# A hand-written order from the first instruction on, edge lists along it, output transposes later, and part of p v on ScalarE, in a graph attention kernel

## Chip, core and metric

The kernel runs on one core of a Trainium2 chip. The metric is the device time of one execution in microseconds (us), as the median of several runs. The engines are TensorE (PE, with its weight loads as PEld), VectorE (DVE), ScalarE (ACT), GpSimd (POOL) and SyncE (SP). Each works through its own queue in order.

## What is computed

One layer of graph attention with a residual and a layer norm, over 16 batches of 1024 nodes with 512 features, 8 heads of 64. The adjacency matrix is the same for all batches and sparse.

```python
q = (x @ Wq + bq).reshape(b, n, H, HD)      # H = 8, HD = 64
k = (x @ Wk + bk).reshape(b, n, H, HD)
v = (x @ Wv + bv).reshape(b, n, H, HD)
scores = jnp.einsum('bqhd,bkhd->bhqk', q, k) / jnp.sqrt(jnp.float32(HD))
scores = scores + (1.0 - adj)[None, None, :, :] * -1000000000.0
attn = jax.nn.softmax(scores, axis=-1)
out = jnp.einsum('bhqk,bkhd->bqhd', attn, v).reshape(b, n, d)
x = _layernorm(x + out @ Wo + bo, axis=-1)  # x: (16, 1024, 512), adj: (1024, 1024)
```

All arithmetic is in 32-bit floats.

## The kernel before

Because the graph is sparse, the kernel works on edges. The 1024 queries are eight tiles of 128, and the edges of a tile are laid into blocks of 128 edges: 11, 6, 4, 4, 3, 3, 3 and 3 blocks, 37 in a batch and 592 in all.

*Edge lists.* `edges(t)` is a generator that makes, once for all batches, the list of a tile. It loads 128 rows of the adjacency (512 KB, from SP's queue), GpSimd multiplies them by column numbers, and VectorE takes out eight columns a round with a MAX (L284) and masks them (L286): ten rounds for tile 0, two for each other tile. Small matmuls (`poff` L295, `pe` L317) place the edges in blocks; the results are `key_row` and `query_row`, the row numbers to be gathered, and `sums`, a 0/1 matrix for each block, which comes out of transposes (`pof` L335).

*Products of a batch.* `front(b, t)` makes q, k and v of a tile from a transposed x (`transpose_x`, L356): each product is four 128x512 matmuls (L374), here called four units. q and kv go to DRAM as rows (`q_rows`, `kv_rows`, two buffers of each, so that one batch is written while another is read), and norms of q and k are collected on the way (squares on ScalarE L385, sums on VectorE L386). When the last tile is done, `mean_v` takes the mean of v by a matmul (`pm`), writes it behind the rows and sets `set_up[b]`; from then on the batch may be gathered.

*Blocks.* For block n, `gather` issues two indirect DMAs from GpSimd (q rows L495, kv rows L500), up to eight blocks ahead. `scores` multiplies q and k on VectorE (L509) and sums by head (L511), `exponentials` runs on ScalarE (L516), `weigh` multiplies v by the eight exponentials on VectorE (L520), and `add_up` adds the block to its queries by two matmuls with `sums` (L532, L533). Behind the last block of a tile `normalise` divides (o, L544), four transposes (`poT`, L553) turn the result, ScalarE copies it (oT), and the tile counts as done.

*Output.* `load_y` loads x again for a tile that is done, GpSimd adds the bias (L455), and `finish` multiplies by Wo (`po`, four units), adds y (L462), takes the layer norm's statistics (L465 to L468), the root on GpSimd (L471 to L473), scales on ScalarE (L476) and stores (L477). The loads of x and y and all stores stand in SP's queue in the order in which they are written.

*What sets the order.* Up to the first block a scheduler places the instructions: the lists of tiles 0 and 1, the bias products and all of batch 0's products. From there on the order is the one in which the program writes them (`tc.manual_schedule`). A loop over steps n puts into step n: the gathers up to n + 8, `weigh(n + 1)`, `scores(n + 2)`, what was put off to this step by `later(k, ...)`, `exponentials(n + 2)`, `add_up(n)`, and then units of other work for a credit of `share`, 3.165 a step (a unit costs 0.86, a group of transposes 0.44): first the units of the next batch's products, and only when these are used up the output products of tiles that are done. The lists of tiles 2 to 7 start at steps 1, 5, 9, 12, 15 and 18 and take one stage a step. Line numbers here and below are those of the kernel before.

## Time and profile before

| | us |
|---|---|
| median of 3 runs | 2704.92 (2704.65 to 2707.9) |
| the profiled execution | 2707.88 |
| its span, first to last instruction | 2706.1 |
| busy in the span: PE / DVE / ACT / POOL | 2507.0 / 2004.2 / 614.3 / 1531.2 |
| granted TensorE clock, mean | 0.966 |

The span cut into 40 equal slices of 67.7 us shows where each engine is busy; a digit is the busy share of a slice in tenths (9 is 90% or more), and the fifth row is the granted clock of TensorE in tenths of full speed:

```profile
PE   4978989999999999999999999999999999999866
PEld 2434545555555555555555555555554555555433
DVE  6358867777787777878777787867777787777775
ACT  2223222222222222222222222222222222222111
POOL 1055564746556474656647475564746566474773
PEclk8988999999999999999999999999999999999878
DMA  3266688787878878787888878787787878788773
```

PE is full in the middle, not in the first five slices and not in the last two. There its clock is below full speed as well.

### The profile page before, as it was taken

How to read it: one execution, taken by the hardware profiler on the slowest of the kernel's cores; microseconds unless marked ns; L12 is line 12 of the kernel's file. 1: busy time of each engine (PE TensorE's matmuls, PEld its weight loads, DVE VectorE, ACT ScalarE, POOL GpSimd, SP SyncE). 2: the span in 40 equal slices, each digit the busy share in tenths (PEclk: the TensorE clock that was granted, in tenths of full speed). 3: DMA queues.
4: the chain of work that ended last, by engine and by line, in shares of the span. 5: the costliest groups of instructions: out<-in, count | busy, mean ns of one | idle time of the engine just before them, and what ended most of it. 6: DMA issues, size and time to landing. Idle time of an engine off the chain costs nothing.

```text
span 2706.1 us, 26468 instructions
## 1 busy us (share of the span) xinstructions
PE 2507.0 (93%) x7659; PEld 1376.4 (51%) x7659; DVE 2004.2 (74%) x3655; ACT 614.3 (23%) x1428; POOL 1531.2 (57%) x1717
## 2 busy tenths in 40 slices
PE   4978989999999999999999999999999999999866
PEld 2434545555555555555555555555554555555433
DVE  6358867777787777878777787867777787777775
ACT  2223222222222222222222222222222222222111
POOL 1055564746556474656647475564746566474773
PEclk8988999999999999999999999999999999999878
DMA  3266688787878878787888878787787878788773
GB/s 124 89 225 230 229 276 270 254 275 250 285 252 281 267 255 275 245 286 253 282 262 267 265 248 288 251 279 263 265 272 237 284 254 286 264 271 252 237 264 112
DMA packets 228679, 678.02 MB, mean 251 GB/s; under 512 B 29454, under 2 KB 29466, under 8 KB 228524
## 3 DMA queue, kind: packets, MB, share of 16 engines
q0 software_dynamic: 132608, 465.64, 54.9%
q1 hardware_dynamic: 93344, 205.60, 20.1%
q10 hardware_dynamic: 2572, 4.99, 0.5%
q8 instruction: 63, 1.03, 0.2%
q14 instruction: 92, 0.75, 0.1%
HBM read 541.86 MB, written 134.25 MB: 250 GB/s over the span
## 4 chain that ended last, share of the span: by engine, by line
PE 71%; DVE 13%; POOL 7%; issue 6%; DMA 2%; ACT 1%; SPq 0%; POOLq 0%; DVEq 0%; ACTq 0%
PE pv L374 16%; PE pk L374 14%; PE pq L374 14%; PE po L374 8%; PE sum L533 7%; PE sum L532 7%; POOL kvg L500 3%; DVE pv L520 3%; DVE qg L509 2%; PE pxT L356 2%; DVE y L462 2%; DVE stats L465 2%; POOL qg L495 2%; PE poT L553 2%; DVE s L511 2%
## 5 line engine op out<-in xcount | busy, mean ns | idle before, releaser
L495 POOL DMA_INDIRECT qg<-q_rows,query_row x592 | 589.1, 995 | 781.0 <-DVE s L511 558.4
L500 POOL DMA_INDIRECT kvg<-kv_rows,key_row x592 | 592.0, 1000 | 194.4 <-issue 192.9
L520 DVE TENSOR_TENSOR pv<-kvg,pv 128x512 f32<-128x512 f32 x592 | 431.9, 730 | 265.5 <-ACT pv L516 236.4
L374 PE MATMUL pv<-wv,xT 128*128 128x512 f32 x1024 | 488.2, 606 | 0.3 <-DVE q L394 0.3
L374 PE MATMUL pk<-wk,xT 128*128 128x512 f32 x1024 | 479.3, 597 | 4.5 <-ACT kv L407 4.5
L374 PE MATMUL pq<-wq,xT 128*128 128x512 f32 x1024 | 482.0, 597 | 0.0
L374 PE MATMUL po<-wo,oT 128*128 128x512 f32 x1024 | 469.6, 599 | 0.0
L509 DVE TENSOR_TENSOR qg<-qg,kvg 128x512 f32<-128x512 f32 x592 | 427.0, 721 | 11.6 <-DMA kvg<-kv_rows,key_row 11.6
L511 DVE TENSOR_REDUCE s<-qg 128x8 f32<-128x512 f32 x592 | 406.2, 686 | 20.5
L532 PE MATMUL sum<-pv,sums 128*128 128x256 f32 x1184 | 368.8, 394 | 26.1 <-DVE pv L520 26.1
L533 PE MATMUL sum<-pv,sums 128*128 128x264 f32 x1184 | 374.3, 399 | 0.0
L516 ACT ACTIVATE pv<-s 128x8 f32<-128x8 f32 x592 | 124.4, 210 | 1082.3 <-DVE s L511 636.9
L532 PEld LDWEIGHTS sum<-pv,sums 128*128 128x128 f32 x1184 | 218.0, 196 | 237.8 <-issue 193.6
L374 PEld LDWEIGHTS pv<-wv,xT 128*128 128x128 f32 x1024 | 201.1, 196 | 205.8 <-issue 195.0
L374 PEld LDWEIGHTS pk<-wk,xT 128*128 128x128 f32 x1024 | 196.1, 192 | 208.7 <-issue 195.1
L374 PEld LDWEIGHTS po<-wo,oT 128*128 128x128 f32 x1024 | 196.9, 193 | 190.3 <-issue 178.6
L374 PEld LDWEIGHTS pq<-wq,xT 128*128 128x128 f32 x1024 | 187.8, 192 | 144.2 <-issue 136.1
L533 PEld LDWEIGHTS sum<-pv,sums 128*128 128x128 f32 x1184 | 232.9, 197 | 34.0
L462 DVE TENSOR_TENSOR y<-po,y 128x512 f32<-128x512 f32 x128 | 87.9, 687 | 152.5 <-POOL y L455 105.8
L455 POOL TENSOR_TENSOR y<-y,bo_bc 128x512 f32<-128x512 f32 x128 | 164.7, 1287 | 57.2 <-DMA y<-in_x_dram 50.9
L553 PE MATMUL poT<-ident,o 128*128 128x128 f32 x512 | 86.4, 293 | 109.5 <-DVE o L544 105.1
L386 DVE TENSOR_REDUCE nrm<-sq 128x8 f32<-128x512 f32 x256 | 172.0, 676 | 12.0 <-ACT sq L385 12.0
(97 smaller groups left out, 1624.0 us busy)
## 6 DMA issues: line engine op xcount, KB each, us to landing
kv_rows<-kv SPq DMA_DIRECT2D x128, 512.0 KB
x<-in_x_dram SPq DMA_DIRECT2D x128, 256.0 KB
q_rows<-q SPq DMA_DIRECT2D x128, 256.0 KB
y<-in_x_dram SPq DMA_DIRECT2D x128, 256.0 KB
out_dram<-y SPq DMA_DIRECT2D x128, 256.0 KB
qg<-q_rows,query_row POOLq DMA_INDIRECT x592
kvg<-kv_rows,key_row POOLq DMA_INDIRECT x592
a<-in_adj_dram SPq DMA_DIRECT2D x8, 512.0 KB
```

The source lines that it names most:

```text
L374: nc.tensor.matmul(p, lhs()[:, ts(c, P)], w[:, c, :], start=(c == 0), stop=(c == NPAIR - 1))
L386: later(1, lambda: nc.vector.tensor_reduce(NRM[b][:, i, t, :], sq.rearrange("p (h d) -> p h d", d=HD), axis=AX.X, op=OP.add))
L455: later(2, lambda: nc.gpsimd.tensor_tensor(Y[b, t], Y[b, t], bo_bc, op=OP.add))
L462: nc.vector.tensor_tensor(y, p, y, op=OP.add)
L495: nc.gpsimd.indirect_dma_start(out=QG[n], out_offset=None, in_=q_rows[b % 2], in_offset=bass.IndirectOffsetOnAxis(ap=query_row[:, g:g + 1] ...
L500: nc.gpsimd.indirect_dma_start(out=KG[n], out_offset=None, in_=kv_rows[b % 2], in_offset=bass.IndirectOffsetOnAxis(ap=key_row[:, g:g + 1], ...
L509: nc.vector.tensor_tensor(m, m, KG[n][:, 0:D], op=OP.mult)
L511: nc.vector.tensor_reduce(S[n], m.rearrange("p (h d) -> p h d", d=HD), axis=AX.X, op=OP.add)
L520: nc.vector.tensor_tensor(pv[:, 0:D].rearrange("p (h d) -> p h d", d=HD), v[:, D:].rearrange("p (h d) -> p h d", d=HD), pv[:, D:, None].to ...
L532: nc.tensor.matmul(SUM[b, t][:, 0, 0:HD2], m, pv[:, 0:HD2], **kw)
L533: nc.tensor.matmul(SUM[b, t][:, 1, 0:HD2 + HEADS], m, pv[:, HD2:], **kw)
L553: nc.tensor.transpose(p[:, ts(c, P)], o[:, ts(c, P)], ident)
```

## The change

The instructions and their sizes stay, but for a part of `weigh`. There are five edits.

1. The hand-written order starts at the first instruction, at step -34, and nothing is left to the scheduler. A step below 0 carries a share of 3.45, with the products of batch 0 and then of batch 1. `later` always puts off.
2. The edge lists start at steps -34, -16, -12, -8, -4, 0, 5 and 10, with one round of MAX and mask a step. The bias products are a generator too, from step -26 on.
3. The share of a step is worked out at each batch's start: all units that are left, over 37 steps. In a middle batch it is 3.07.
4. The transposes `poT` and the mean's matmul go into a list, `urgent`. A step empties it behind its `add_up` and, where product units of a batch are left, behind its first unit.
5. In batch 0 every odd block, and in batch 15 two blocks of three, have `weigh` on ScalarE: eight activations of 128x64, each with one head's exponential as its scale.

```diff
-EDGES_FROM = (0, 0, 1, 5, 9, 12, 15, 18)
+LEAD_IN = 34
+EDGES_FROM = (-34, -16, -12, -8, -4, 0, 5, 10)
+LEAD_SHARE = 3.45
...
         def later(k, fn):
-            if now[0] is None:
-                fn()
-            else:
-                plan.setdefault(now[0] + k, []).append(fn)
+            plan.setdefault(now[0] + k, []).append(fn)
...
                     nc.vector.scalar_tensor_tensor(
                         v, v, kl[:, r * 8 + 7:r * 8 + 8], v, op0=OP.is_lt, op1=OP.mult
                     )
+                    yield
...
             def mean_v():
+                urgent.append(mean_pe)
+
+            def mean_pe():
                 p = fill_psum(f"pm_{b}")
...
         def weigh(n):
             v, pv = KG.pop(n), PV[n]
+            b, t, i = blocks[n]
+            if (b == 0 and n % 2) or (b == B - 1 and n % 3):
+                for h in range(HEADS):
+                    nc.scalar.activation(
+                        pv[:, ts(h, HD)], v[:, ds(D + h * HD, HD)], AF.Copy, scale=pv[:, D + h:D + h + 1]
+                    )
+                return
...
-            later(1, transpose)
+            later(1, lambda: urgent.append(transpose))
...
+                if front_batches < B and front_batches <= max(n // NB, 0) + 1:
+                    fronts += [u for t in range(NT) for u in front(front_batches, t)]
+                    front_batches += 1
+                if n < 0:
+                    share = LEAD_SHARE if n > -LEAD_IN else TRANSPOSE * 1.5
+                elif n % NB == 0:
+                    tiles = len(done) + (NT if n + NB < total else NT + 2)
+                    share = (sum(u[0] for u in fronts) + tiles * NPAIR * PRODUCT) / NB
...
                 credit += share
-                while credit > 0:
+                first_unit = True
+                while credit > 0 or urgent:
+                    if urgent and not (first_unit and fronts):
+                        urgent.pop(0)()
+                        continue
                     if not fronts and not finishing and done and n > loaded.get(done[0], n):
                         finishing = finish(*done.pop(0))
                     units = finishing or fronts
                     if not units:
+                        if urgent:
+                            urgent.pop(0)()
+                            continue
                         break
                     cost, fn = units.pop(0)
                     fn()
                     credit -= cost
+                    first_unit = False
```

Two places on PE and one on SP show what moves. A name such as `po_7_3` is the output product of batch 7's tile 3, `sum_8_0` the sum of batch 8's tile 0, and the last number of a name only counts instructions.

PE at the program's start, before: the x transposes of batch 0, tile 0's edge list in one piece, then the first products.

```order
L254 MATMUL pb3_141<-wo_69,bvb_139 128x512 x4
L356 MATMUL pxT_0_0_147<-ident_58,x_0_0_126 128x128 x4
L356 MATMUL pxT_0_1_156<-ident_58,x_0_1_128 128x128 x4
L295 MATMUL poff_0_196<-est_169,before_100 128x1
L317 MATMUL pe_0_0_206<-kl_0_170,of_0_203 128x82 x6
L317 MATMUL pe_0_6_222<-kl_0_170,of_0_203 128x82 x5
L335 MATMUL pof_0_0_237<-ident_58,of_0_203 128x128 x4
L335 MATMUL pof_0_4_243<-ident_58,of_0_203 128x128 x4
L335 MATMUL pof_0_8_249<-ident_58,of_0_203 128x128 x3
L374 MATMUL pq_0_0_254<-wq_63,xT_0_0_152 128x512 x4
L374 MATMUL pk_0_0_266<-wk_65,xT_0_0_152 128x512 x4
L374 MATMUL pv_0_0_276<-wv_67,xT_0_0_152 128x512 x4
```

PE at the program's start now:

```order
L359 MATMUL pxT_0_0_134<-ident_58,x_0_0_128 128x128 x4
L359 MATMUL pxT_0_1_139<-ident_58,x_0_1_130 128x128 x4
L377 MATMUL pq_0_0_158<-wq_63,xT_0_0_150 128x512 x4
L377 MATMUL pk_0_0_171<-wk_65,xT_0_0_150 128x512 x4
L377 MATMUL pv_0_0_183<-wv_67,xT_0_0_150 128x512 x4
L359 MATMUL pxT_0_2_195<-ident_58,x_0_2_132 128x128 x4
L377 MATMUL pq_0_1_200<-wq_63,xT_0_1_154 128x512 x4
L377 MATMUL pk_0_1_215<-wk_65,xT_0_1_154 128x512 x4
L377 MATMUL pv_0_1_226<-wv_67,xT_0_1_154 128x512 x4
L359 MATMUL pxT_0_3_238<-ident_58,x_0_3_152 128x128 x4
L377 MATMUL pq_0_2_243<-wq_63,xT_0_2_208 128x512 x4
L377 MATMUL pk_0_2_257<-wk_65,xT_0_2_208 128x512 x3
```

The products of batch 0 stand right behind the first two groups of x transposes, and the edge and bias matmuls have gone in between later units.

PE from the transposes of tile 5 to those of tile 6 at the end of batch 7, before:

```order
L553 MATMUL poT_7_5_8951<-ident_58,o_7_5_8918 128x128 x4
L532 MATMUL sum_7_6_8930<-pv_291_8891,sums_108 128x256
L533 MATMUL sum_7_6_8930<-pv_291_8891,sums_108 128x264
L374 MATMUL po_7_3_8937<-wo_69,oT_7_3_8776 128x512 x2
L374 MATMUL po_7_4_8972<-wo_69,oT_7_4_8879 128x512 x2
L532 MATMUL sum_7_6_8930<-pv_292_8928,sums_108 128x256
L533 MATMUL sum_7_6_8930<-pv_292_8928,sums_108 128x264
L374 MATMUL po_7_4_8972<-wo_69,oT_7_4_8879 128x512 x2
L532 MATMUL sum_7_7_9032<-pv_293_8966,sums_108 128x256
L533 MATMUL sum_7_7_9032<-pv_293_8966,sums_108 128x264
L553 MATMUL poT_7_6_9047<-ident_58,o_7_6_9020 128x128 x4
```

The same stretch now:

```order
L566 MATMUL poT_7_5_9071<-ident_58,o_7_5_9023 128x128 x4
L377 MATMUL po_7_2_9042<-wo_69,oT_7_2_8785 128x512 x3
L377 MATMUL po_7_3_9079<-wo_69,oT_7_3_8890 128x512
L545 MATMUL sum_7_6_9035<-pv_292_9033,sums_108 128x256
L546 MATMUL sum_7_6_9035<-pv_292_9033,sums_108 128x264
L377 MATMUL po_7_3_9079<-wo_69,oT_7_3_8890 128x512 x3
L545 MATMUL sum_7_7_9140<-pv_293_9065,sums_108 128x256
L546 MATMUL sum_7_7_9140<-pv_293_9065,sums_108 128x264
L377 MATMUL po_7_4_9145<-wo_69,oT_7_4_8980 128x512 x4
L545 MATMUL sum_7_7_9140<-pv_294_9104,sums_108 128x256
L546 MATMUL sum_7_7_9140<-pv_294_9104,sums_108 128x264
L566 MATMUL poT_7_6_9174<-ident_58,o_7_6_9128 128x128 x4
```

The output products come later, so that eleven units instead of six lie between the two groups of transposes, with three pairs of sums in both. From tile 6's to tile 7's transposes it is twelve units before and now.

SP's queue around the load of y for tile 5 of batch 7, before:

```order
L454 DMA y_7_4_8933<-in_x_dram 128x512
L477 DMA out_0_dram<-y_6_7_8174 128x512
L477 DMA out_0_dram<-y_7_0_8788 128x512
L477 DMA out_0_dram<-y_7_1_8823 128x512
L454 DMA y_7_5_9035<-in_x_dram 128x512
L477 DMA out_0_dram<-y_7_2_8859 128x512
L477 DMA out_0_dram<-y_7_3_8895 128x512
```

and now:

```order
L460 DMA y_7_4_9069<-in_x_dram 128x512
L483 DMA out_0_dram<-y_6_7_8296 128x512
L483 DMA out_0_dram<-y_7_0_8932 128x512
L460 DMA y_7_5_9143<-in_x_dram 128x512
L483 DMA out_0_dram<-y_7_1_8954 128x512
L483 DMA out_0_dram<-y_7_2_8993 128x512
L483 DMA out_0_dram<-y_7_3_9038 128x512
```

The load `y_7_5` stands ahead of the store of `y_7_1` instead of behind it. These places look the same in every batch from the third on.

More of the change, by code (lines that the diff above doesn't have):

```diff
@@ L586 @@
             fronts, finishing = [], []
+            front_batches = 0
             credit = 0.0
-            n = 0
-            for k in range(2):
-                gather(k)
-                gathered += 1
-            scores(0)
-            exponentials(0)
-            weigh(0)
-            scores(1)
-            exponentials(1)
-            while n < total or plan or done or finishing:
-                now[0] = n
-                if n < total and blocks[n][1:] == (0, 0):
-                    b = blocks[n][0]
-                    if b + 1 < B:
-                        fronts = [u for t in range(NT) for u in front(b + 1, t)]
+            for t in range(3):
+                load_x(0, t)
+            fronts += transpose_x(0, 0) + transpose_x(0, 1)
+            n = -LEAD_IN
+            while n < total or plan or urgent or done or finishing:
+                now[0] = n
+                if front_batches < B and front_batches <= max(n // NB, 0) + 1:
[6 more added lines that the diff above has]
+                    share = (sum(u[0] for u in fronts) + tiles * NPAIR * PRODUCT) / NB
                 while gathered < min(n + AHEAD + 1, total) and blocks[gathered][0] in set_up:
@@ L605 @@
                     gathered += 1
-                if n + 1 < total:
+                if 0 <= n + 1 < total:
                     weigh(n + 1)
-                if n + 2 < total:
+                if 0 <= n + 2 < total:
                     scores(n + 2)
```

43 lines of the change are left out of this document (16 added, 27 removed).

## The prediction

> **What bounds the kernel now.** I cut the span at the first sum matmul of batch 0, batch 1, batch 2 and batch 15 (each batch has 37 blocks, so 148 recorded sum matmuls) and asked the view of stretches for each engine's busy time. The columns are the stretch, its length, the busy time and instruction count of PE, PEld, DVE, ACT and POOL, the granted clock, the DMA share and GB/s.
> ```profile
> 0.00:156.40 156.40, 107.25 (x299) 54.06 (x299) 68.50 (x113) 31.37 (x52) 14.07 (x22) 0.93 0.32 113
> 156.40:356.30 199.90, 168.29 (x522) 94.64 (x523) 156.56 (x324) 56.56 (x119) 117.99 (x111) 0.89 0.70 237
> 356.30:508.60 152.30, 150.83 (x471) 82.92 (x471) 119.41 (x216) 35.34 (x84) 90.16 (x101) 1.00 0.81 265
> 508.60:2553.80 2045.20, 1986.37 (x6103) 1088.74 (x6102) 1561.38 (x2811) 470.98 (x1118) 1216.39 (x1383) 0.99 0.81 265
> 2553.80:2706.10 152.30, 94.28 (x267) 56.04 (x265) 98.35 (x193) 20.06 (x56) 92.63 (x104) 0.79 0.59 197
> ```
> So the span is 156.4 (lead-in) + 199.9 (batch 0) + 152.3 (batch 1) + 2045.2 (batches 2 to 14, 157.3 each) + 152.3 (batch 15) = 2706.1 us. TensorE is the bound in the middle: 150.83 of 152.3 us busy in batch 1. In the lead-in, batch 0 and batch 15 no engine is full, and those are the stretches that the change rewrites. The price of a piece of PE work comes from the timeline (start, length, engine, line; two records make one matmul).
> ```profile
> 1239.86 2.74 PE L374 MATMUL pq<-wq,xT 128*128 128x512 f32 x6
> 1242.44 1.02 PE L374 MATMUL pk<-wk,xT 128*128 128x512 f32 x2
> 1243.30 0.59 PE L532 MATMUL sum<-pv,sums 128*128 128x256 f32 x2
> 1244.17 2.74 PE L374 MATMUL pk<-wk,xT 128*128 128x512 f32 x6
> 1251.06 0.60 PE L553 MATMUL poT<-ident,o 128*128 128x128 f32 x4
> 1251.49 0.60 PE L532 MATMUL sum<-pv,sums 128*128 128x256 f32 x2
> ```
> Start to start, a unit (one 128x512 matmul) is (1242.44 - 1239.86)/3 = 0.86 us, a block's pair of sums 0.87, a group of four transposes 0.43. A full batch is 128 units, 37 sums and 16 groups: 110.1 + 32.2 + 6.9 = 149.2 us, beside batch 1's 150.83 of PE work. A later batch is 157.3, so it loses about 6.5 us. The table of waits and the timeline say where.
> ```profile
> PE poT L553 <- DVE o L544: 105.1, 33, 10.6
> 973.23 0.77 PE L553 MATMUL poT<-ident,o 128*128 128x128 f32 x4 [1.45 <-DVE o L544]
> 984.86 0.69 DVE L462 TENSOR_TENSOR y<-po,y 128x512 f32<-128x512 f32 x1 [5.36 <-POOL y L455]
> 989.52 0.68 PE L553 MATMUL poT<-ident,o 128*128 128x128 f32 x4 [2.60 <-DVE o L544]
> 973.00:976.00 3.00, 2.77 (x12) 1.81 (x13) 2.90 (x8) 0.50 (x1) 2.51 (x3) 1.00 0.62 212
> 990.80:994.20 3.40, 3.40 (x6) 1.43 (x5) 3.33 (x7) 2.43 (x5) 2.79 (x3) 0.51 0.71 167
> ```
> At each end of a batch PE, in order, waits at the output transposes of the last two tiles for VectorE's o: 1.45 and 2.60 us. VectorE is late because its y waits 5.36 us for GpSimd. After the longer gap the clock is 0.51 for 3.4 us, which costs another 1.7; after the short gap it stayed 1.00. That is 5.75 of the 6.5.
>
> On the clock, the Trainium skill ("TensorE: Matmul & The Clock Gate", Part 1) says that the array falls to half rate after an idle window of about 3.4 us. This trace disagrees: 2.60 us of idling were enough for the 0.51 above. By the rule the 1.7 would not come back, which would make the sum below about 14 x 1.7 = 24 us longer, 2603 us; the measured row decides.
>
> **The change, part by part. Batches 1 to 14.** Their PE work is the same. The batch's share is now spread over all 37 steps, so the last output products come later: between the transposes of tile 5 and those of tile 6, PE had 6 units and now has 11, with three pairs of sums in both; from tile 6 to tile 7 it has 12 in both. VectorE therefore gets 5 x 0.86 = 4.3 us more before PE asks for o. Against this stands about one more tile to finish inside the same stretch:
> ```profile
> L462 DVE TENSOR_TENSOR y<-po,y 128x512 f32<-128x512 f32 x128 | 87.9, 687 | 152.5 <-POOL y L455 105.8
> L465 DVE BATCH_NORM_STATS2 stats<-y 128x6 f32<-128x512 f32 x128 | 88.9, 695 | 4.4
> L466 DVE BATCH_NORM_AGGREGATE mv<-stats 128x2 f32<-128x6 f32 x128 | 23.3, 182 | 4.3
> L468 DVE TENSOR_SCALAR rstd<-mv 128x1 f32<-128x1 f32 x128 | 19.6, 154 | 4.4
> ```
> The columns of this listing are line, engine, operation, tiles, shapes and count, then busy us in all, mean ns of one, and idle time before it. The four make 0.69 + 0.70 + 0.18 + 0.15 = 1.7 us. Net cover is 2.6 against gaps of 4.05, so I leave a gap of 1.45, short enough (row 973.00) for the clock to stay up. The load of y for tile 5 also stands one output store earlier in SP's queue, which can only shorten VectorE's 5.36. A batch becomes 150.8 + 1.45 = 152.25; bounds are 150.8 (no gap) and 157.3 (all as before). Fourteen batches: 2131.5 instead of 2197.5, **66 us less**.
>
> **Lead-in.** What starts it, and what it holds:
> ```profile
> 17.83 1.28 ACT L280 ACT_TABLE_LOAD   x1 [17.83 <-DMA bq_bc<-in_L_gnn_bq_dram]
> 50.44 1.89 PE L374 MATMUL pq<-wq,xT 128*128 128x512 f32 x2
> L284 DVE MAX8 kl<-codes 128x8 f32<-128x1024 f32 x24 | 29.4, 1227 | 35.8 <-POOL codes L274 35.5
> L286 DVE SCALAR_TENSOR_TENSOR codes<-codes,kl 128x1024 f32<-128x1024 f32 x16 | 20.5, 1283 | 0.3
> L335 PE MATMUL pof<-ident,of 128*128 128x128 f32 x37 | 7.7, 355 | 1.9 <-ACT kv L407 1.9
> L317 PE MATMUL pe<-kl,of 128*128 128x18 f32 x52 | 6.5, 257 | 2.7 <-DVE of L308 2.0 <-DVE q L394 0.6
> ```
> ScalarE is issuing DMAs until 17.83 us and loads its table until 19.1; only then can it copy the first x transposes (0.6 us), so the first product moves from 50.44 to 19.7 us, ahead of the edge lists instead of behind them. Ten rounds of tile 0's list (1.23 + 1.28 = 2.5 us each) now stand one in a step of 4 units. Before the first sum PE now has 128 units (all of batch 0 and two and two thirds tiles of batch 1) = 110.1, 12 groups of transposes = 5.2, the bias products 4 x 0.86 = 3.4, and the edge work of tiles 0 to 3 and half of 4, about 14 (an estimate: the two rows with tile 0's wider gathers and the offsets make some 20 us for 37 blocks, and 26 blocks lie here): 133 us. In the first ten steps VectorE has 2.5 us of rounds and about 1.1 of a tile's work per step against PE's 3.44, so it loses 0.2 a step, and PE's in-order waits and a cold start cost some more: I add 6. The first gathers stand four steps, 14 us of PE work, ahead of the first sum, and the adjacency loads on SP behind the stores of q and kv, a step or more ahead of their use; what they take longer than that adds to the 159. The lead-in is 19.7 + 133 + 6 = 159 us, between 152 (nothing added) and 175 (each round costs a wait of 2 us). That is **2.5 us more**, but with 32 units (27.5 us) of batch 1 done.
>
> **Batch 0.** Before, VectorE was busy 156.56 of 199.9 us, 78%, since six edge lists and all of batch 1's products lay there. Moved out: two and two thirds lists at 8 us (two MAX, one masking pass of 1.28, some twenty small ones: 21), as many tiles of batch 1 at 3.4 us (q, k, two norms and one v sum, five pieces of 0.68: 9), and 18 products of p and v that ScalarE takes over:
> ```profile
> L394 DVE SCALAR_TENSOR_TENSOR q<-pq,bq_bc 128x512 f32<-128x512 f32 x128 | 87.7, 685 | 35.1 <-PE pq L374 35.1
> L386 DVE TENSOR_REDUCE nrm<-sq 128x8 f32<-128x512 f32 x256 | 172.0, 676 | 12.0 <-ACT sq L385 12.0
> L520 DVE TENSOR_TENSOR pv<-kvg,pv 128x512 f32<-128x512 f32 x592 | 431.9, 730 | 265.5 <-ACT pv L516 236.4
> L516 ACT ACTIVATE pv<-s 128x8 f32<-128x8 f32 x592 | 124.4, 210 | 1082.3 <-DVE s L511 636.9
> L407 ACT COPY kv<-pv 128x512 f32<-128x512 f32 x128 | 74.9, 585 | 286.7 <-PE pv L374 280.2 <-issue 6.5
> L476 ACT ACTIVATE y<-y,rstd 128x512 f32<-128x512 f32 x128 | 102.8, 803 | 56.5 <-POOL rstd L473 56.4 <-issue 0.2
> ```
> 18 x 0.73 = 13. So 156.6 - 43 = 113.5 us of VectorE; at the same 78% the batch takes **145 us, 55 less**. PE has 88 units, 37 sums, 13 groups and the last edges there, 118 us, which is the lower bound; the upper is 175, if edges stay as obstructive as before. The price of one 128x64 activation is not in the trace: above the 128x8 one (0.21) and below the 128x512 one with two pointers (0.80). On the line from 128x8 to the copy of 128x512 it is 0.21 + 56/504 x 0.375 = 0.25, near the small row; eight make 2.0 us a block. Behind the eight pieces on ScalarE stand the x copies, for which PE waits, and the next exponentials, for which VectorE's even blocks wait; 2.0 us fits into a step of 3.9. ScalarE then works 57 + 36 = 93 of 145 us; at 0.80 it would be 57 + 116 = 173, and become the bound.
>
> **Batch 15.** The rows of gathers, of the last gather and of the last sum:
> ```profile
> L495 POOL DMA_INDIRECT qg<-q_rows,query_row x592 | 589.1, 995 | 781.0 <-DVE s L511 558.4
> L500 POOL DMA_INDIRECT kvg<-kv_rows,key_row x592 | 592.0, 1000 | 194.4 <-issue 192.9
> 2653.14 1.17 POOL L495 DMA_INDIRECT qg<-q_rows,query_row  x1 [0.50 <-issue]
> 2654.62 0.95 POOL L500 DMA_INDIRECT kvg<-kv_rows,key_row  x1 [0.30 <-issue]
> 2683.27 0.59 PE L532 MATMUL sum<-pv,sums 128*128 128x256 f32 x2
> ```
> To 2653 GpSimd works without a pause longer than its issue: 29 blocks at 2.0 + 0.6 us and six tiles' y and roots. The change takes nothing from GpSimd, so these 99 us stay, and the relief of VectorE there is worth nothing. Behind the last gather it is worth something: 30.1 us to the last sum hold eight blocks, of which five shed 0.73 us on VectorE (3.7), and PE no longer puts all four units of a tile at once before a sum, 3.44 us each time; two such waits less make 6.9. 30.1 - 3.7 - 6.9 = 19.5, so 20. The tail of 22.8 us gets 2 to 3 longer, since more products are left over. 99 + 20 + 25 + 1 = **145, 7 less**; bounds 134 and 170 (ScalarE at 0.80 per piece).
>
> **Sum.** 159 + 145 + 2131.5 + 145 = 2580.5 us of span, 125.6 below 2706.1. The profiled execution took 2707.88, 1.78 more than its span, and lay 2.96 above the median of 2704.92; so 2580.5 + 1.8 - 3.0 = 2579 us on the median's scale.
>
> **Rivals.** (1) The wait at the transposes only moves: the last group is passed by one pair of sums and one unit, and the cover goes to the later finish. Then batches stay at 157.0 on the mean, 14 x 4.75 = 66 us more: 2646. For it speaks that VectorE's lateness comes from GpSimd, not from PE; against it the 11 units. (2) Hand order from the start stalls: PE meets each edge step in order, with one step of slack. With 175 us for the lead-in and 170 for batch 0 the time is 2620. For it speaks batch 0's 78%, where the same stages lay among the same units. (3) It turns slower: finishing eight tiles at an even pace makes GpSimd the bound of that phase. Rows:
> ```profile
> 964.22 1.28 POOL L455 TENSOR_TENSOR y<-y,bo_bc 128x512 f32<-128x512 f32 x1
> 969.84 1.28 POOL L455 TENSOR_TENSOR y<-y,bo_bc 128x512 f32<-128x512 f32 x1
> ```
> One block and one finish take GpSimd 5.62 us, a step of 3.6 units takes PE 4.1. If its lead of eight gathers no longer covers this, eight finishes cost 8 x 1.5 = 12.2 us a batch: 163, 2730 us in all. It decides from (2706.1 - 449)/14 = 161.2 us a batch on. Against it: GpSimd was busy only 90 of 152 us. (4) Nothing net changes, for gains and waits cancel.
>
> **How the numbers follow.** Forecast 2579 (some 2530 to 2610) 0.66; rival 1 0.16; rival 2 0.12; rival 3 0.04; rival 4 0.02. The range 2530 to 2645 holds the forecast, rival 2 and half of rival 1. A measurement tells 0.2% (5 us) from no change; faster 0.94, same 0.02, slower 0.04.
>
> **What would show it.** The first product near 20 us and the first sum of batch 0 near 159; batch 1 starting near 304; the wait of poT for o well under 105 us, with few 0.5 clocks between batches 1 and 14 and 152 us between first sums; ScalarE's 128x64 pieces near 0.25 us; the last gather 99 us after batch 15's first sum. Wrong would be a piece over 0.5 us, a lead-in over 175, or batches still at 157.

## The result, and the profile after

| | before | after |
|---|---|---|
| median of 4 runs | 2706.41 us (2704.65 to 2710.72) | 2596.93 us (2592.49 to 2598.53) |
| ratio, with its 95% interval | | 0.9591 [0.9573, 0.9608] |
| the profiled execution | 2707.88 us | 2595.89 us |
| its span | 2706.1 us | 2594.1 us |
| mean granted clock | 0.966 | 0.982 |

The forecast was 2579 us in a range of 2530 to 2645. On the page of the changed kernel, the span in 40 slices of 64.9 us has PE at nine tenths or more from the fifth slice on (before: from the seventh), and only the last two slices below; the clock is below nine tenths in three slices, before in six.

Cut as before, at the first sum matmul of batches 0, 1, 2 and 15, the changed kernel has these stretches (the view of stretches, with the same columns):

```profile
0.00:162.40 162.40, 136.76 (x401) 67.10 (x402) 92.67 (x172) 47.69 (x84) 32.57 (x36) 0.98 0.44 155
162.40:309.50 147.10, 127.28 (x423) 73.60 (x422) 118.42 (x247) 73.40 (x232) 96.67 (x97) 0.92 0.79 269
309.50:460.00 150.50, 150.50 (x471) 82.90 (x470) 117.47 (x215) 34.80 (x83) 85.81 (x97) 1.00 0.81 268
460.00:2458.50 1998.50, 1969.48 (x6103) 1078.71 (x6102) 1554.12 (x2811) 474.37 (x1116) 1195.44 (x1379) 1.00 0.81 271
2458.50:2594.10 135.60, 93.61 (x267) 50.27 (x266) 85.51 (x171) 68.40 (x250) 88.55 (x112) 0.81 0.68 227
```

| stretch | before | forecast | after | after less forecast |
|---|---|---|---|---|
| lead-in | 156.4 | 159 | 162.4 | +3.4 |
| batch 0 | 199.9 | 145 | 147.1 | +2.1 |
| batches 1 to 14 | 2197.5 | 2131.5 | 2149.0 | +17.5 |
| batch 15 | 152.3 | 145 | 135.6 | -9.4 |
| span | 2706.1 | 2580.5 | 2594.1 | +13.6 |

Of the 112.0 us, batch 0 gave 52.8, batches 1 to 14 gave 48.5 and batch 15 gave 16.7; the lead-in took 6.0. PE is busy without a gap in batch 1 (150.50 of 150.50 us), but a batch from 2 to 14 takes 1998.5 / 13 = 153.7 us. The table of waits shows what stands where the wait of poT stood. From here on line numbers are those of the changed kernel: poT is L566, o L557, VectorE's y L468, GpSimd's y L461, pv L533 on VectorE and L529 on ScalarE, the sums L545 and L546.

```profile
DVE y L468 <- POOL y L461: 139.4, 64, 5.4
PE sum L545 <- DVE pv L533: 33.8, 21, 2.4
PE poT L566 <- DVE o L557: 11.2, 13, 5.6
```

poT's wait fell from 105.1 to 11.2 us. The sums' wait for pv takes its place at the start of a batch, and VectorE's wait for GpSimd's y, its source before, grew from 105.8 to 139.4 us. The timeline around the first sum of batch 4 shows the whole chain of that new wait, on four engines, in order of time:

```profile
755.97 0.38 SPq L460 DMA_DIRECT2D y<-in_x_dram  x1
760.79 9.64 SPq L483 DMA_DIRECT2D out_dram<-y  x3
762.93 1.27 POOL L461 TENSOR_TENSOR y<-y,bo_bc 128x512 f32<-128x512 f32 x1
770.48 0.68 SPq L460 DMA_DIRECT2D y<-in_x_dram  x1
771.07 0.94 POOL L506 DMA_INDIRECT kvg<-kv_rows,key_row  x1 [0.30 <-issue]
772.04 1.27 POOL L461 TENSOR_TENSOR y<-y,bo_bc 128x512 f32<-128x512 f32 x1
773.35 0.69 DVE L468 TENSOR_TENSOR y<-po,y 128x512 f32<-128x512 f32 x1 [5.36 <-POOL y L461]
775.09 0.68 DVE L533 TENSOR_TENSOR pv<-kvg,pv 128x512 f32<-128x512 f32 x1
775.83 0.70 PE L545 MATMUL sum<-pv,sums 128*128 128x256 f32 x2 [1.89 <-DVE pv L533]
```

Read from below: PE idles 1.89 us for pv of the batch's second block. On VectorE pv stands behind a tile's y, which waited 5.36 us for GpSimd's addition. By the program's order this is the addition for tile 5 of batch 3, whose output is finished here. The load that it needs was issued at 755.97 and had landed at 760.05, by the semaphore that it sets. The addition follows 12 us later, because in GpSimd's order it stands behind the gathers of two more blocks (the last of them at 771.07) than the addition for tile 4 (762.93), and GpSimd works through these with pauses of at most 0.51 us. The load at 770.48, which SP held back behind three output stores for 9.64 us, is tile 6's. It landed at 775.87, too late to have a part in this.

So the new wait looks like one of a queue's order, GpSimd's: the load is asked for when a tile counts as finished, and the addition is written two steps behind that, behind the gathers of those steps. Twelve runs test this and the other steps. Each was timed against the kernel before; times below are medians of four runs, to be held against 2596.9 for the change. Lengths of stretches are those of one profiled execution of each run. Where the same stretch is the same program in several runs, they differ by this much: the lead-in 160.3 to 162.7 us (eight executions), batch 0 147.1 to 148.2 (four), batch 15 134.6 to 138.1 (four).

### The profile page after: what moved, and what is told of

Read it like the earlier page. It is cut to its first block, busy times and chain, and to the rows that moved or that the text cites. A ratio compares the mean times of both kernels' runs of the same rounds, so it can differ in the third digit from the quotient of the medians.

```text
span 2594.1 us, 26742 instructions
## 1 busy us (share of the span) xinstructions
PE 2477.6 (96%) x7659; PEld 1352.6 (52%) x7659; DVE 1968.2 (76%) x3613; ACT 698.7 (27%) x1764; POOL 1499.0 (58%) x1717
## 4 chain that ended last, share of the span: by engine, by line
PE 68%; POOL 11%; DVE 10%; issue 7%; ACT 2%; DMA 1%; ACTq 0%; POOLq 0%; another core or an unknown queue 0%; SPq 0%; DVEq 0%
PE pv L377 16%; PE pk L377 15%; PE pq L377 15%; PE sum L546 7%; PE sum L545 7%; POOL kvg L506 4%; PE po L377 4%; POOL y L461 3%; POOL qg L501 2%; DVE y L468 2%; DVE stats L471 2%; PE pxT L359 2%; PE poT L566 2%; DVE qg L515 1%; DVE pv L533 1%
## 5 line engine op out<-in xcount | busy, mean ns | idle before, releaser
L533 DVE TENSOR_TENSOR pv<-kvg,pv 128x512 f32<-128x512 f32 x550 | 394.3, 717 | 223.1 <-ACT pv L522 146.8
L377 PE MATMUL pk<-wk,xT 128*128 128x512 f32 x1024 | 488.9, 598 | 7.1 <-ACT xT L363 7.1
L377 PE MATMUL pv<-wv,xT 128*128 128x512 f32 x1024 | 479.1, 593 | 0.0
L515 DVE TENSOR_TENSOR qg<-qg,kvg 128x512 f32<-128x512 f32 x592 | 432.6, 731 | 0.3 <-issue 0.3
L545 PE MATMUL sum<-pv,sums 128*128 128x256 f32 x1184 | 361.6, 387 | 46.4 <-DVE pv L533 33.8
L545 PEld LDWEIGHTS sum<-pv,sums 128*128 128x128 f32 x1184 | 222.2, 192 | 326.5 <-issue 239.0
L546 PE MATMUL sum<-pv,sums 128*128 128x264 f32 x1184 | 366.6, 392 | 4.6 <-ACT pv L529 2.3
L377 PEld LDWEIGHTS pv<-wv,xT 128*128 128x128 f32 x1024 | 190.5, 191 | 167.0 <-issue 158.4
L546 PEld LDWEIGHTS sum<-pv,sums 128*128 128x128 f32 x1184 | 226.2, 192 | 41.6 <-ACT pv L529 6.4
L461 POOL TENSOR_TENSOR y<-y,bo_bc 128x512 f32<-128x512 f32 x128 | 163.4, 1277 | 141.5 <-ACT pv L522 74.7
L468 DVE TENSOR_TENSOR y<-po,y 128x512 f32<-128x512 f32 x128 | 88.0, 688 | 151.5 <-POOL y L461 139.4
L404 DVE TENSOR_TENSOR kv<-pk,bk_bc 128x512 f32<-128x512 f32 x128 | 88.2, 689 | 115.8 <-PE pk L377 87.2
```

What stands on the lines that cost most here:

```text
L377: nc.tensor.matmul(p, lhs()[:, ts(c, P)], w[:, c, :], start=(c == 0), stop=(c == NPAIR - 1))
L461: later(2, lambda: nc.gpsimd.tensor_tensor(Y[b, t], Y[b, t], bo_bc, op=OP.add))
L468: nc.vector.tensor_tensor(y, p, y, op=OP.add)
L515: nc.vector.tensor_tensor(m, m, KG[n][:, 0:D], op=OP.mult)
L533: nc.vector.tensor_tensor(pv[:, 0:D].rearrange("p (h d) -> p h d", d=HD), v[:, D:].rearrange("p (h d) -> p h d", d=HD), pv[:, D:, None].to ...
L545: nc.tensor.matmul(SUM[b, t][:, 0, 0:HD2], m, pv[:, 0:HD2], **kw)
```

## The experiments: batches 1 to 14

**The output transposes at their old place** (edit 4 undone for poT).

```diff
-            later(1, lambda: urgent.append(transpose))
+            later(1, transpose)
```

> The changed kernel with one part undone: the output transposes stand again ahead of the sums of their step. Theory (moving them back is what took the wait of poT away, beside the more even share): PE meets poT before the second block's sums and before o is there, about 4.0 us of idling at the start of a batch in place of 1.88 + 0.18, and the clock falls behind it in most batches (1.7 us): 2 to 3.7 us a batch, 2597 + 28 to 52 = 2625 to 2649 us. Rival (the 11 units of the even share did it alone, the new place is worth nothing): 2592 to 2602 us, and no wait of poT over 1 us.

Measured: 2641.6 us, 44.7 more; batches 2 to 14 take 156.8 on the mean. The timeline of the same place, with VectorE's y ahead of it:

```profile
781.77 0.69 DVE L468 TENSOR_TENSOR y<-po,y 128x512 f32<-128x512 f32 x1 [5.36 <-POOL y L461]
786.43 0.69 PE L566 MATMUL poT<-ident,o 128*128 128x128 f32 x4 [4.07 <-DVE o L557]
```

One wait of 4.07 us stands where the kernel before had 1.45 and 2.60, together 4.05, and VectorE's y waits 5.36 us for GpSimd as in the change. With the even share alone, then, the wait is as long as before; the place of the transposes is worth 156.8 - 153.7 = 3.1 of the 3.6 us that a batch gained.

**The share of a step as before** (edit 3 undone in batches 1 to 13).

```diff
                     share = (sum(u[0] for u in fronts) + tiles * NPAIR * PRODUCT) / NB
+                    if 0 < n < total - 2 * NB:
+                        share = NT * (4 * NPAIR * PRODUCT + 2 * TRANSPOSE) / NB
```

> The changed kernel with the share of a step in batches 1 to 13 again as before, 3.165 us instead of 3.070, so that the output products end sooner; the transposes stay where the change puts them. Theory of the prediction (the more even share puts 11 units for 6 between the last transposes and so gives VectorE 4.3 us): without it 3 us or more of waiting come back in each batch, 156 us or more, 2630 us or more. Rival (with the transposes at their old place and the even share a batch took 156.6, so the place is worth 3.1 us of the 3.8 and the share 0.7 at most): 2597 to 2607 us, batches 153.3 to 154.2.

Measured: 2600.2 us, ratio 0.9605 [0.958, 0.9629], which overlaps that of the change: no difference that this can tell. Batches stay at 154.1, and the wait at their start is 2.15 to 2.72 us in place of 1.88 + 0.18. The 4.3 us of cover that the prediction drew from the even share were not there.

**y loaded for three finished tiles instead of two.**

```diff
-                for tile_done in done[:2]:
+                for tile_done in done[:3]:
```

> The changed kernel, but y of a tile is loaded when it is among the first three finished ones, not the first two, so GpSimd adds the bias to it a step earlier. Theory (in the finishing phase GpSimd needs 5.2 us a step against some 4.5 of PE, VectorE's y waits for GpSimd's y in the same step, pv of the second block stands behind it, and PE loses 2.1 us there, with about 1 more behind it): batches 2 to 14 go from 153.5 to 151, 13 x 2.5 = 33 less, 2564 us (2558 to 2575). Rival 1 (the two gathers of a block set GpSimd's pace wherever y stands): 2592 to 2602. Rival 2 (the seven y buffers run out, SP waits for an output store with stores of q and kv queued behind): over 2602.

Measured: 2595.5 us, ratio 0.958 [0.9557, 0.9603]: no difference. This miss was instructive. When tile 5 joins the list of finished tiles, the list is nearly empty, so a third place in it moves nothing for this tile. In GpSimd's order the addition for tile 4 moves ahead, but that for tile 5 stays behind the same gathers as in the change, and VectorE's longest wait for y was 8.7 us.

**y asked for when a tile's sums are normalised,** three steps before it counts as finished; the first added line stands in `normalise`.

```diff
+            soon.append((b, t))
...
-                for tile_done in done[:2]:
+                for tile_done in soon[:2]:
...
+                        soon.remove(done[0])
                         finishing = finish(*done.pop(0))
```

> The changed kernel, but the load of a tile's y is asked for when its sums are normalised, three steps before its output transposes are copied; still two at a time. Theory (tile 6 comes last into the list of finished tiles, so its load of y is written last, and stands on SP behind output stores that wait for ScalarE, 9.6 us in the steady state; GpSimd's y, VectorE's y, pv of the second block and PE follow from it): the 1.88 + 0.18 us go from the starts of batches 2 to 14, and the three falls of the clock with them: 13 x 2.1 + 3 x 1.7 = 32 less, 2565 us (2558 to 2572), batches at 151. Rival (GpSimd's 5.2 us per step of the finishing phase, two gathers, y and roots, makes VectorE late whenever y was loaded): 2592 to 2602 us.

Measured: 2555.3 us, 41.6 less, ratio 0.9432 [0.941, 0.9454]. First the view of stretches for batches 2 to 14, then the timeline at the start of batch 4:

```profile
454.10:2417.11 1963.01, 1960.41 (x6103) 1077.68 (x6103) 1571.59 (x2811) 474.13 (x1116) 1199.27 (x1378) 1.00 0.82 276
```
```profile
752.04 1.27 POOL L461 TENSOR_TENSOR y<-y,bo_bc 128x512 f32<-128x512 f32 x1
756.22 0.96 POOL L506 DMA_INDIRECT kvg<-kv_rows,key_row  x1 [0.30 <-issue]
757.21 1.27 POOL L461 TENSOR_TENSOR y<-y,bo_bc 128x512 f32<-128x512 f32 x1
758.51 0.69 DVE L468 TENSOR_TENSOR y<-po,y 128x512 f32<-128x512 f32 x1 [1.42 <-POOL y L461]
762.88 0.59 PE L545 MATMUL sum<-pv,sums 128*128 128x256 f32 x2
```

PE is busy for 1960.41 of 1963.01 us, a batch takes 151.0, and the second block's sums (762.88) wait for nothing. The addition for tile 5 (757.21) now stands behind the gathers of one block instead of two and starts 5.2 us after that for tile 4 (752.04), in the change 9.1. GpSimd's y still costs VectorE 1.42 us in a step, and that does no harm: GpSimd's pace of 5.2 us a step, the rival, does not by itself make PE wait. The edit was right, but the reason that the expectation gives for it is not what the traces show: the load behind the three stores is tile 6's, and the load for tile 5 had landed 12 us before its addition already in the change. What counts is that the addition moves ahead in GpSimd's order together with the load. No run moves one of the two alone. Of the 44.9 us between the two spans, 35.3 lie in batches 1 to 14; batch 0 gave 4.2, batch 15 3.5, and the lead-in 2.0.

**The same edit in the kernel before the change.**

> The kernel before the change, with one edit that the change doesn't have: y asked for when a tile's sums are normalised. Theory (before, too, the wait of poT for o at the start of a batch comes from tile 6's load of y standing late on SP): gaps of 1.45 and 2.60 and the half clock go from each of 14 batches, 157.3 to 151.5, 2708 - 81 = 2627 us (2615 to 2640), lead-in and batch 0 as before. Rival (at the old place PE is ahead of VectorE's o by the place alone, and GpSimd's y is half of it at most): 2660 us or more.

Measured: 2669.8 us, ratio 0.9867 [0.9834, 0.9899]: between the two. Batches 2 to 14 fall from 157.3 to 155.3, not to 151.5. poT's wait has left the head of the table of waits, but the sums wait for pv at the end of batches instead, 0.80 and 2.60 us in six batches and one wait of 2.03 to 4.02 in the other seven. At a share of 3.165 the units of a batch are used up early, and steps without any follow.

**Early y and the old share together,** in the changed kernel.

> The changed kernel with two edits: y asked for three steps sooner (2555 us by itself) and the share of batches 1 to 13 again at 3.165 us (3 us by itself, 2600). Theory (the even share is worth something only once y is no longer late: with 3.165 some steps have no unit between two pairs of sums, and PE then waits for VectorE's pv, 0.80 + 2.60 us at the end of a batch in the old kernel with the same early y): batches of 153 to 156, 2585 to 2625 us. Rival (the place of the transposes does all of it, the share is worth 3 us here too): 2552 to 2562 us, batches of 151.

Measured: 2600.3 us, ratio 0.9609 [0.9582, 0.9637], 45 us more than with early y alone; batches 2 to 14 at 154.0. The timeline at the end of a batch shows how (poT's line is one higher here):

```profile
764.42 0.60 PE L567 MATMUL poT<-ident,o 128*128 128x128 f32 x4
764.86 0.60 PE L545 MATMUL sum<-pv,sums 128*128 128x256 f32 x2
765.30 0.61 PE L546 MATMUL sum<-pv,sums 128*128 128x264 f32 x2
767.96 0.67 PE L545 MATMUL sum<-pv,sums 128*128 128x256 f32 x2 [2.05 <-DVE pv L533]
```

Two pairs of sums and the transposes stand one behind the other without a unit, PE runs through them, and VectorE's pv is 2.05 us late. The even share is thus worth nothing that shows while y is late, and 45 us once y is early. Early y in turn is worth 41.6 us with the even share and nothing without it (2600.2 and 2600.3).

## The experiments: lead-in, batch 0, batch 15

**The first two x tiles copied by VectorE.**

```diff
-                    nc.scalar.copy(XT[b, t], p)
+                    copy = nc.vector.tensor_copy if b == 0 and t < 2 else nc.scalar.copy
+                    copy(XT[b, t], p)
```

> The changed kernel, but VectorE copies the first two transposed x tiles, not ScalarE, which issues DMAs until 19.95 us. Theory (the 13.2 us for which the first product waits are a term of the lead-in by themselves): first product near 10 us in place of 21.9, lead-in 162.4 - 8 to 12, 2585 to 2589 us. Rival (the ten masking rounds of tile 0 on VectorE, 2.5 us each, and the edge steps behind them set the end of the lead-in, PE only waits later): lead-in 159 to 163, 2592 to 2600 us.

Measured: 2585.9 us, 11.0 less; the first sum comes at 151.5 us. The timeline's first microseconds, of the change, then of this run (whose lines behind the edit are one higher):

```profile
19.95 1.28 ACT L363 ACT_TABLE_LOAD   x1 [19.95 <-DMA bk_bc<-in_L_gnn_bk_dram]
21.88 6.62 PE L377 MATMUL pq<-wq,xT 128*128 128x512 f32 x8 [13.18 <-ACT xT L363]
```
```profile
8.49 4.61 PE L378 MATMUL pq<-wq,xT 128*128 128x512 f32 x8
```

The first product starts 13.4 us earlier, and 10.9 of them arrive at the first sum. VectorE's masking rounds, the rival, do not set the lead-in's end.

**The edge lists of tiles 2 to 7 at their old steps.**

```diff
-EDGES_FROM = (-34, -16, -12, -8, -4, 0, 5, 10)
+EDGES_FROM = (-34, -16, 1, 5, 9, 12, 15, 18)
```

> The changed kernel with the edge lists of tiles 2 to 7 again at the steps of before (1, 5, 9, 12, 15, 18 of batch 0), those of tiles 0 and 1 as changed. Theory of the prediction (two and two thirds lists are 21 us of VectorE's work, 27 us of batch 0 at 78%, and cost little ahead of it): lead-in 6 to 10 shorter, batch 0 25 to 30 longer, 2597 + 15 to 24 = 2612 to 2621 us. Rival (a list costs the same wherever it stands, since PE waits for its loads and passes in the lead-in too): 2592 to 2602 us.

Measured: 2602.5 us, 5.6 more, ratio 0.9603 [0.9581, 0.9625], which overlaps that of the change; just above the rival's upper end. Its lead-in and batch 0 in the view of stretches:

```profile
0.00:149.80 149.80, 130.05 (x371) 62.58 (x372) 76.66 (x127) 38.05 (x71) 22.38 (x31) 1.00 0.42 149
149.80:315.75 165.95, 139.79 (x452) 80.96 (x450) 137.03 (x291) 84.06 (x244) 106.81 (x102) 0.90 0.76 256
```

Spreading the lists makes batch 0 18.9 us shorter (165.95 to 147.1) and the lead-in 12.6 longer (149.8 to 162.4). Most of it only moves: with the spread of the lead-in, 10.5 to 12.9 of the 18.9 us.

**Adjacency tiles loaded two steps ahead of the rest of their list.** In the end of the lead-in and in batch 0 of the change PE waits three times for a copy on ScalarE, 4.45 us at 155.90, 5.89 at 178.30 and 7.15 at 222.80. The second of these, in order of time:

```profile
162.59 0.42 SPq L274 DMA_DIRECT2D a<-in_adj_dram  x1
169.88 2.35 POOL L276 TENSOR_TENSOR codes<-a,place 128x1024 f32<-128x1024 f32 x1 [7.04 <-DMA a<-in_adj_dram]
172.27 1.06 ACT L282 ACTIVATE a<-a 128x1024 f32<-128x1024 f32 x1 [4.37 <-POOL codes L276]
175.78 2.00 ACT L529 ACTIVATE pv<-kvg,pv 128x64 f32<-128x64 f32 x8
177.68 0.56 ACT L410 COPY kv<-pv 128x512 f32<-128x512 f32 x1
178.30 0.90 PE L338 MATMUL pof<-ident,of 128*128 128x128 f32 x3 [5.89 <-ACT kv L410]
```

The load of the adjacency is issued at 162.59 and read by GpSimd only 7 us later; ScalarE's pass over the tile waits for that, then come the eight pieces of p v, and the copy that frees PE's PSUM buffer stands last.

```diff
-EDGES_FROM = (-34, -16, -12, -8, -4, 0, 5, 10)
+EDGES_FROM = (-34, -18, -14, -10, -6, -2, 3, 8)
...
         nc.sync.dma_start(a, adj[ds(t * P, P), :])
+            for _ in range(2 if t else 0):
+                yield
```

> The changed kernel, but each adjacency tile after the first is loaded two steps ahead of the rest of its edge list, which keeps its steps. Theory (in the lead-in's end and batch 0, GpSimd's codes wait for that load, ScalarE's three passes over the tile wait for the codes, and kv and xT copies stand behind them; PE then waits 4.45, 5.89 and 7.15 us): these go, with half a clock of 6.8 us behind each: 15 to 27 less, 2570 to 2582 us. Rival (VectorE's masking rounds, two lists at once, hold the same stages): first sum of batch 0 within 2 us of 162, batch 0 at 144 or more, 2590 to 2600 us.

Measured: 2582.5 us, 14.5 less, ratio 0.9534 [0.9512, 0.9557]. The lead-in is 158.7 and batch 0 137.5 us; PE's three waits shrink from 4.45, 5.89 and 7.15 to 3.29, 3.10 and 1.05. They do not vanish: ScalarE's three passes over a tile still stand ahead of its copies.

**p v on VectorE in all blocks** (edit 5 undone).

```diff
-            if (b == 0 and n % 2) or (b == B - 1 and n % 3):
+            if False:
```

> The changed kernel with p v on VectorE in all blocks, ScalarE's pieces undone. Theory of the prediction (18 blocks x 0.73 us at 78% in batch 0 = 17 us, 3.7 us behind the last gather of batch 15): 2597 + 21 = 2618 us, of which 4 in batch 15. Rival 1 (batch 15, measured 9.4 us shorter than forecast, owes this to ScalarE's 24 blocks): batch 15 at 149 or more, 2627 us. Rival 2 (eight pieces of 0.33 us hold up ScalarE's copies, for which PE waits 4.5 and 5.9 and 7.2 us in batch 0): batch 0 gets shorter by 5 to 10, 2590 to 2595 us.

Measured: 2601.6 us, 4.6 more, ratio 0.9605 [0.9586, 0.9625], which overlaps that of the change. Batch 0 and batch 15 in the view of stretches:

```profile
160.33:307.56 147.23, 128.44 (x423) 73.55 (x422) 130.10 (x266) 40.96 (x93) 95.62 (x97) 0.94 0.79 271
2455.58:2599.00 143.42, 90.64 (x267) 50.93 (x266) 99.29 (x195) 22.13 (x58) 96.66 (x111) 0.82 0.66 215
```

In batch 0 VectorE has 11.7 us more to do (130.10 to 118.42) and the batch is as long as with ScalarE's help, 147.23 to 147.1. That does not mean that neither engine matters there. PE waits for other things: its wait for VectorE's pv that ends at 198.05 is 2.16 us long (0.33 in the change), its wait for ScalarE's xT that ends at 221.07 is 2.23 (7.15 in the change). Of PE's waits over 0.2 us in batch 0, those that ScalarE ends fall from 13.6 to 7.0 us without its pieces, and those that VectorE ends rise from 6.2 to 11.7. In these waits gain and price of the help cancel.

Batch 15 gets 7.8 us longer, and at 143.4 lies outside the 134.6 to 138.1 of the runs that leave it as it is. Where in batch 15 does the help count?

**In batch 15 on ScalarE only in the last eight blocks.**

```diff
-            if (b == 0 and n % 2) or (b == B - 1 and n % 3):
+            if (b == 0 and n % 2) or (n >= len(blocks) - 8 and n % 3):
```

> The changed kernel with ScalarE's share of p v in batch 15 kept for the last eight blocks alone; batch 0 as changed. Theory of the prediction (GpSimd sets the pace up to the last gather, so relief of VectorE counts only behind it): 2593 to 2599 us, last gather 97 us after the batch's first sum. Rival (GpSimd's gathers wait for the qg buffers that VectorE frees, so the relief ahead of the last gather is what counts; without any the last gather came 103.4 us after): last gather at 101 to 104 us, 2600 to 2604 us.

Measured: 2602.2 us, ratio 0.9609 [0.9586, 0.9632], which overlaps that of the change; batch 15 at 142.0. The view of stretches from the batch's first sum to the end of its last gather, for the change, for the run without any help, and for this run:

```profile
2458.54:2556.59 98.05, 65.64 (x185) 35.72 (x185) 63.04 (x119) 52.83 (x202) 75.56 (x88) 0.79 0.84 278
2455.58:2559.90 104.32, 63.30 (x184) 36.73 (x184) 74.44 (x138) 14.10 (x42) 84.42 (x88) 0.79 0.81 261
2459.21:2563.83 104.62, 64.90 (x185) 38.52 (x185) 74.09 (x138) 16.12 (x50) 85.03 (x88) 0.79 0.81 260
```

The help ahead of the last gather brings it some 6 us forward (98.05 to 104.62; in the three other runs that leave batch 15 as it is, it ends after 97.1 to 100.9). Behind it the help is worth about 1.5 at most: with all of it the last sum comes 18.3 us behind the start of the last gather (here 18.1), without it 19.8.

So the rival's number came out, but not its wait. GpSimd's 88 instructions are the same in all three rows. It is idle for 22.5, 19.9 and 19.6 us, so it does not wait longer for VectorE's buffers; it is busy for 75.56, 84.42 and 85.03 us. The instructions themselves last longer: a gather of kv rows 0.98 us on the mean in the change, 1.14 without any help and 1.17 here. Why they do is not shown; in batches 2 to 14, where VectorE also does p v in all blocks, such a gather takes 0.99 us.

**Three edits together:** VectorE's two copies, the early adjacency loads, and early y.

> The changed kernel with three edits together: VectorE copies the first two x tiles (11.0 us by its own run), adjacency loads two steps earlier (21 forecast), y asked for three steps sooner (32 forecast). If the three are separate terms: 2597 - 64 = 2533 us (2520 to 2550). If VectorE is what the lead-in and batch 0 then wait for, so that the first two don't add up: 2550 to 2570 us.

Measured: 2531.7 us, ratio 0.9341 [0.932, 0.9363]; it beats both kernels, and gains 65.2 us, where the three terms of 11.0, 14.5 and 41.6 us add up to 67.1. Its lead-in and batch 0 take 147.59 and 137.59 us; batches 2 to 14:

```profile
438.06:2401.97 1963.91, 1960.33 (x6103) 1077.68 (x6103) 1566.04 (x2811) 474.66 (x1116) 1197.49 (x1379) 1.00 0.82 276
```

## Why the prediction was right, and where not

The total came out 18 us above the forecast, and part of that closeness is luck: batches 1 to 14 are 17.5 us too long and batch 15 is 9.4 too short, and they have different causes.

*Batches 1 to 14: right in the direction, 17.5 us too low, and wrong in the reason.* The prediction followed poT's wait of 2.60 us back to VectorE's y and to GpSimd, and so far it holds. In the kernel before, the gathers of three blocks stand between GpSimd's additions for tiles 4 and 5 of batch 4:

```profile
969.84 1.28 POOL L455 TENSOR_TENSOR y<-y,bo_bc 128x512 f32<-128x512 f32 x1
983.55 1.27 POOL L455 TENSOR_TENSOR y<-y,bo_bc 128x512 f32<-128x512 f32 x1
```

But it held that o is late by a fixed 1.45 and 2.60 us and that 11 units in place of 6 give it 4.3 us. With the transposes at their old place those units gave nothing, and undoing the share alone cost nothing that shows. What PE meets is a date set by GpSimd's order: the addition for tile 5 stands behind the gathers of the steps in which it is written, and VectorE's wait for it is 5.36 us in the kernel before, in the change, and with the transposes moved back. The load of y that stands one store earlier on SP shortened nothing, since it was not late. The step that failed is "net cover is 2.6 against gaps of 4.05": cover was counted in units of PE, while the late thing hung on another queue. The moved transposes helped (3.1 us a batch), as it seems because PE does more work before it needs o; then PE met the same late y at the sums ahead of poT, through pv. That is rival 1, "the wait only moves", in a weaker form, and what spoke for it, that the lateness comes from GpSimd and not from PE, was right: 2.06 us of waiting in a batch are left, where the forecast left 1.45. Of the 17.5 us these are 13 x 2.06 - 14 x 1.45 = 6.5, and three falls of the clock, 1.7 each, another 5; the remaining 6 were not told apart. The base of 150.8 was right; early y gives 151.0.

*Lead-in: right.* The order of events was as told, with the first product at 21.88 for 19.7 us: ScalarE was issuing DMAs until 19.95, not 17.83. These 2.2 us are most of the 3.4, though the lead-in of the same program spreads from 160.3 to 162.7. That the wait for ScalarE is a term by itself is shown by the run with VectorE's copies.

*Batch 0: right in the sum (147.1 for 145), wrong in its parts.* Of the 55 us, the prediction gave VectorE's relief by ScalarE 13 / 0.78 = 17, and the lists 21 / 0.78 = 27. Measured, the first is 0 and the second 18.9, of which the lead-in pays 12.6. "At the same 78%" failed: the length does not follow VectorE's work, for 11.7 us more of it, given back by ScalarE, leave the batch as long. For ScalarE's copies the prediction charged nothing ("2.0 us fits into a step of 3.9"); in PE's waits the help gives 5.5 us on VectorE and costs 6.6 on ScalarE. At least part of what is waited for is the adjacency load, through ScalarE, worth 9.6 us of batch 0. The other 34 us, from 199.9 to the 165.95 with the lists at their old steps, go with the work of batch 1 that is already done in the lead-in; that part was not tried by itself, so it stays argued, and that the sum came within 2.1 us is luck.

*Batch 15: 9.4 us better than forecast, in three terms.* The forecast's 99 us end at the start of the last gather of q rows (row 2653.14). Counted so, it came after 95.9 for 99 us, the last sum 19.5 for 20 behind it, and the rest took 20.2 for 25 + 1. Two steps failed. One is "the relief of VectorE there is worth nothing": GpSimd does set the pace, as the prediction says, but its instructions last longer without the relief, and that gather then comes after 101.9 us. That the forecast of 99 was near is luck: ScalarE's help made up for a batch that without it would have been later than before. The other is the tail: it was to get 2 to 3 us longer than 22.8 and got 2.6 shorter, which is the largest of the three terms; why was not tried.

*ScalarE's price: right.* A piece of 128x64 lasts 0.333 us by itself (the median of 336), but eight in a row take 2.00 us (row 175.78), 0.25 each, as the line between the two rows had given. The Trainium skill ("ScalarE: Activation LUTs", What ACT_TABLE_LOAD costs) gives 186 ns + 0.833 ns an element + 93 ns for a pointer operand, less 93 where activations follow each other: as an estimate 332 ns alone and 239 in a row. The rows have 333 and 250, and agree.

*The other rivals.* The stall of the hand order (2) was there in a small form, 14.5 us by the early adjacency loads. GpSimd's pace in the finishing phase (3) shows in the run with early y, where its y start at 752.04 and 757.21, 5.2 us apart, and VectorE waits 1.42 us for each; but PE's sums don't wait there, and the pace alone decides nothing. It matters through the place of the addition for tile 5, which is why a step sooner was worth 41.6 us.

## What to carry to other kernels

Work that waits for almost nothing, here a load and the addition behind it, should be written into an in-order queue ahead of other work, when its buffer is free and not when its consumer is next. Before a late transfer is blamed, look up which tile it carries and when it landed: the views leave out tile numbers, and the held-up load next to the wait was another tile's. Two parts of a change can hide each other: undoing one alone may show nothing, while undoing it beside the repair of the other wait shows 45 us. An engine that is busy 69% of a stretch (VectorE in batch 15 without relief, 99.29 of 143.42 us) can still be worth relieving, without any wait that the trace names: with its relief undone, the same 88 instructions kept GpSimd busy for 84.42 us in place of 75.56. So relief is priced by a run without it, not by a busy share, and a run that shows no difference may hold a gain and a price that cancel, as in batch 0.

## What the runs showed of the clock

The forecast expected the clock to stay up after short gaps. Gaps of 1.88 to 1.90 us stand at the start of batches 2 to 14, and the clock fell after three of them. Two such gaps end at 2006.18 and at 929.33 us, both 1.90 us long by PE's rows of the timeline. Here is the view of stretches around each, cut at multiples of 3.41 us from each other:

```profile
2004.10:2007.51 3.41, 1.51 (x6) 1.06 (x6) 3.27 (x8) 0.00 (x0) 2.44 (x5) 1.00 0.65 210
2007.51:2010.92 3.41, 3.41 (x8) 1.71 (x7) 3.31 (x8) 1.28 (x4) 2.80 (x5) 0.50 0.82 248
925.46:928.87 3.41, 1.98 (x5) 0.57 (x3) 1.92 (x5) 0.00 (x0) 2.72 (x6) 1.00 0.87 281
928.87:932.28 3.41, 2.77 (x11) 1.73 (x12) 3.31 (x9) 0.91 (x2) 2.92 (x5) 1.00 0.50 125
```

The first gap lies in one cell of the grid, PE is busy 1.51 of 3.41 us in it, and the next cell has a clock of 0.50. The second is split by the grid, 1.98 us stay busy, and the clock holds. In the 14 profiled executions of this study each fall of the clock starts on such a grid of 3.413 us, counted from the first fall of that execution. Of PE's gaps of 1.0 to 4.5 us between 460 and 2330 us, those with less than 1.80 us in any cell made the clock fall in 5 of 104 cases (all five had a second gap of 0.8 us just ahead in the same cell, 1.76 to 2.08 us together); with 1.95 us or more it was 36 of 39, and in between 12 of 24. So it is not a gap's length that counts but the idle time in one cell, and in these executions the limit is near 1.9 us. The Trainium skill ("TensorE: Matmul & The Clock Gate", Part 1) tells of a free-running window of 3413 ns, which the grid confirms, and of one idle window before the rate halves, which the rows deny: a window 55% idle was enough.
